# A four-layer graph network: where the next unit's row is spread in PSUM

## The chip, the cores and the metric

The kernel runs on one core of a Trainium2 chip. The metric is device microseconds (us) of one execution. A core has five engines that run side by side and wait for each other through semaphores: PE (TensorE, matrix products), DVE (VectorE), ACT (ScalarE), POOL (GpSimd) and SP (SyncE, which here issues DMAs). PE writes its results into PSUM; DVE and ACT read them there.

## The reference

The input is `x`, 8 images of 2048 nodes with 64 features, and `adj`, one 2048x2048 adjacency matrix that all images and layers share. Four layers follow each other, each as `x = layernorm(x + layer(x, adj))`.

Layers 0, 1 and 2 are graph attention. With `h = x @ W`, `s1 = h @ a1`, `s2 = h @ a2`:

```python
e = leaky_relu(s1[:, :, None] + s2[:, None, :], negative_slope=0.2)
att = softmax(where(adj > 0, e, very_negative), axis=-1)
out = att @ h          # then elu (layers 0, 1) or relu (layer 2)
```

Layer 0 scales the nodes first and normalizes `h`. Layer 3 has no scores between nodes: it takes `feat = softplus(...)`, weights it by `exp(feat * wa + ba)` and averages it over each node's neighbours, so it is one product of the mask with numerators and denominators.

## The kernel before, in words

**Units and tiles.** For layers 0 to 2 a unit is one image in one layer. The list `todo` has 24: layers 0 and 1 of images 0 to 3 (units 0 to 7), the same of images 4 to 7 (units 8 to 15), and layer 2 of all images (units 16 to 23). A unit has K = 16 tiles `jb`; a tile holds 128 neighbours (on the partitions) against all 2048 nodes (along the free axis). Layers 0 and 1 are "the first two layers" and layer 2 "the third layer" below.

**A tile.** `weights(u, jb)` is one DVE instruction: it takes the larger of the unit's row `r` and a number per partition, times the mask `edge`, and writes `w` (128x2048). The first and last tile of a unit are done in two halves (`halves`), so that what waits for one half can go on. In the third layer `exponential` then puts `w` through Exp on ACT; in the first two layers the weights are already exponentials. `products(u, jb)` multiplies the tile by the values (`pv`, or `x` in the third layer) on PE and adds into two PSUM banks `acc`; the profile counts two passes for fp32, so a tile has 8 matmul instructions. After the sixteenth tile four small matmuls add the mean for nodes without neighbours. There are 4 buffers for `w`.

**The row.** The row of a unit is the same on all partitions. It lies in DRAM as three bf16 parts whose sum is the fp32 value; `prepare` loads them into SBUF ahead of time, at step 10 of the unit before or later, as soon as they are ready. `spread` (line 830) brings them to all partitions: four matmuls of 128x512 with ones as the stationary operand write four PSUM banks, `r`. There is one such `r` for all units from 1 on (`psR`, one buffer). So a unit's row can be spread only when the last weights of the unit before have read the old one, and the next unit's first weights can start only after it.

**Order of the work.** All compute instructions go through `InOrder`, which keeps each engine's instructions in the order in which the program issues them; that helper is line 80 of the file, and the profile therefore shows line 80 for nearly all of them. DMAs on SP are placed by the framework.

The main loop goes over units and tiles. A step `t = K*n + jb` does this in order: `reach(t)`, `products(u, jb)`, possibly `prepare` for the next unit, and `bg.step()`. `bg.step()` advances the side work: generators for everything else (the end of the unit before, the next layer's scores, features of later images, in the third layer also layer 3's products `p_l`), each of which issues a piece per step.

`reach(t)` (line 1013) issues weights as far as they may run ahead of the products: in the first two layers those of tile `t`, in the third layer those up to tile `t + 2`. In the third layer it then issues exponentials up to tile `t + 1`. When it has issued a unit's last weights (`jb == K - 1`) and the next unit's row is prepared, it calls `spread_for(n + 1)` at once (line 1025). `spread_for` does nothing for a unit that has its row already; a unit whose row wasn't spread by then gets it just before its first weights.

So in the program's order, the spread stood after the last weights and before the sixteenth tile's products in the first two layers (step 15), and after the last weights and before the fourteenth tile's products in the third layer (step 13, since weights run two tiles ahead).

Of the kernel before, what the change touches and what calls it, by code (L numbers as in the profile page):

```python
# [50 lines left out]
def gnn4_kernel(ctx: ExitStack, tc: tile.TileContext, t, out):  # L51
# [3 lines left out]
    K = N // P  # L55
# [224 lines left out]
    def mask(p, jb):  # L280

        for h in range(2):
            dve.tensor_scalar(
                edge[:, jb, h * (N // 2) : (h + 1) * (N // 2)],
                raws[jb][h], 0.0, None, ALU.is_gt, saturate=False,
            )
        if jb < 6:
            load_raw(jb + 6)
        elif jb >= 10:
            load_raw(jb + 2)  # L290
        if jb == K2:
            load_x(2)
        if jb >= K - 3:
            load_x(jb - K + 6)
        if jb == 0:
            pe.matmul(p[:, : 2 * K], lhsT=edge[:, 0, :P], rhs=zeros_h, start=True, stop=False)
        for ib in range(K):
            pe.matmul(
                p[:, 2 * ib : 2 * ib + 2],
                lhsT=edge[:, jb, ib * P : (ib + 1) * P],  # L300
                rhs=ones_h,
                start=False,
                stop=False,
            )
        if jb == K - 1:
            pe.matmul(p[:, : 2 * K], lhsT=edge[:, 0, :P], rhs=zeros_h, start=False, stop=True)
# [21 lines left out]
    def empties(p):  # L328
        deg = p[:, : 2 * K : 2]
        dve.tensor_scalar(empty, deg, 0.0, None, ALU.is_equal)  # L330

        dve.tensor_scalar(
            half_ldeg, deg.bitcast(I32), 0.5 * LN2 / (1 << 23), LSE_UP - 63.5 * LN2,
            ALU.mult, ALU.add,
        )

        em = tmp.tile([P, 4, NCH, 32], F32, tag="oT", name="em")
        dve.tensor_copy(
            em,
            empty.rearrange("p (c k) -> p k c", k=4)[:, :, :, None].to_broadcast([P, 4, NCH, 32]),  # L340
        )
        q = Banks.pool.tile([P, 512], F32, tag="b", name="p_empty")
        for k in range(4):
            pe.transpose(
                q[:, k * P : (k + 1) * P], em[:, k].rearrange("p c b -> p (c b)"), ident
            )
        dve.tensor_copy(emptyT, q)
# [482 lines left out]
    def spread(layer, b):  # L830

        sc = S[layer, b]
        sc.r = Banks.r
        for c in range(NCH):
            sl = slice(c * 512, (c + 1) * 512)
            pe.matmul(sc.r[:, sl], lhsT=ones3, rhs=sc.r3[:, sl], start=True, stop=True)
# [134 lines left out]
    def unit(layer, b):  # L971
        u = Unit()
        u.layer, u.b, u.n = layer, b, f"{layer}_{b}"
        u.s, u.w = S[layer, b], {}
        return u

    def sums_of(u):
        u.acc = [psA.tile([P, 512], F32, tag="acc", name=f"acc_{u.n}_{c}") for c in range(2)]
# [5 lines left out]
    def weights(u, jb):  # L984

        s = u.s
        w = u.w[jb] = work.tile([P, N], F32, tag="w", name=f"w_{u.n}_{jb}", bufs=4)
        low = s.low if u.layer == 2 else s.e[:, 1]
        for sl in halves(u, jb):
            dve.scalar_tensor_tensor(  # L990
                w[:, sl], s.r[:, sl], low[:, jb : jb + 1], edge[:, jb, sl], ALU.max, ALU.mult
            )

    def exponential(u, jb):

        w = u.w[jb]
        for sl in halves(u, jb):
            act.activation(w[:, sl], w[:, sl], AF.Exp, bias=u.s.down[:, jb : jb + 1])

    units, prepared, spreads = [], set(), {0}  # L1000

    def spread_for(n):
        if n in spreads:
            return
        spreads.add(n)
        if n == 1:
            Banks.use("psR", 1)
            Banks.r = Banks.pool.tile([P, N], F32, tag="b", name="r")
        spread(*todo[n])
# [3 lines left out]
    def reach(t):  # L1013

        while front[0] < K * len(todo):
            n, jb = divmod(front[0], K)
            layer, b = todo[n]
            if n not in prepared or front[0] > t + (2 if layer == 2 else 0):
                break
            if jb == 0:  # L1020
                spread_for(n)
                units.append(unit(layer, b))
            weights(units[n], jb)
            front[0] += 1
            if jb == K - 1 and n + 1 in prepared:
                spread_for(n + 1)
        while behind[0] < min(front[0], t + 2):
            n, jb = divmod(behind[0], K)
            if todo[n][0] == 2:
                exponential(units[n], jb)  # L1030
            behind[0] += 1

    def products(u, jb):

        s, w = u.s, u.w[jb]
        sums = [u.acc[c // 2][F * (c % 2) : F * (c % 2) + F, :] for c in range(NCH)]
        for c in range(NCH):
            pe.matmul(
                sums[c],
                lhsT=s.v[:, jb, :],  # L1040
                rhs=w[:, c * 512 : (c + 1) * 512],
                start=(jb == 0),
                stop=False,
            )
        if jb == K - 1:

            assert s.whole
            for c in range(NCH):
                rows = slice(32 * c, 32 * c + 3)
                pe.matmul(sums[c], lhsT=s.mean[rows], rhs=emptyT[rows], start=False, stop=True)  # L1050
# [337 lines left out]
    def chain(*gens):  # L1388
        for g in gens:
            if isinstance(g, int):  # L1390
                yield g
            else:
                yield from g()
# [26 lines left out]
    def flags():  # L1420

        for layer in range(2):
            dve.tensor_scalar(s_top[:, layer], s_top[:, layer], -S_MAX[layer], None, ALU.add)
        top = small.tile([P, 2], F32, tag="top", name="top")
        dve.tensor_reduce(top[:, 0:1], s_top, AX.XY, ALU.max)
        yield 1
        yield from pm_slots.take()
        p = psum("p_top")
        pe.transpose(p[:1, :P], top[:, 0:1], ident)
        yield 1  # L1430
        dve.tensor_reduce(top[0:1, 1:2], p[:1, :P], AX.X, ALU.max)
        pm_slots.give()
        dve.tensor_tensor(beyond[0:1, :], beyond[0:1, :], top[0:1, 1:2], ALU.max)
        dve.tensor_scalar(flag, beyond[0:1, :], 0.0, None, ALU.is_gt)
# [3 lines left out]
    for n, (layer, b) in enumerate(todo):  # L1438
        if (layer, b) == (2, 1):
            early_.close()  # L1440
            late = ctx.enter_context(tc.tile_pool(name="late", bufs=1))
            bg.add(l3_products())
        if (layer, b) == (2, 5):
            bg.add(flags())
        now[:] = layer, n, 0
        nxt = todo[n + 1] if n + 1 < len(todo) else None
        done = nxt is None

        for jb in range(K):
            if n == 0:  # L1450
                while masks < min(K, 9 + jb):
                    mask(p_deg, masks)
                    masks += 1
                if jb == K - 3:
                    empties(p_deg)
            now[2] = jb
            reach(K * n + jb)
            u = units[n]
            if jb == 0:
                sums_of(u)  # L1460
            products(u, jb)
            if jb == K - 1:
                end = [lambda u=u: finish(u)]
                if layer < 2:
                    end += [2 if now[0] < 2 else 1, lambda layer=layer, b=b: scores(layer + 1, b)]
                else:
                    end += [1, lambda b=b: l3_features(b)]
                if layer == 1 and b % NB == NB - 1:
                    end += [lambda b=b: group(b // NB)]
                bg.add(chain(*end), begun=True)  # L1470
            elif not done and jb >= 10 and ready(*nxt):
                prepare(*nxt)
                prepared.add(n + 1)
                done = True
            if layer == 0 and jb == 2 and 6 <= b + 4 < B:
                load_x(b + 4)
            if n == 0 and jb == 3:
                bg.add(constants())
            if n == 9 and jb == 3:
                bg.add(mask_out())  # L1480
            if (n, jb) in begin:
                bg.add(features0(begin[n, jb]))
            bg.step()
        while not done:
            bg.step()
            if ready(*nxt):
                prepare(*nxt)
                prepared.add(n + 1)
                done = True
# [509 lines left out]
```

## Time and profile before

| What | Value |
|---|---|
| Median of 3 runs | 1397.81 us (1397.5 to 1398.58) |
| Profiled execution | 1401.63 us |
| Its span, first to last instruction | 1399.8 us |
| Mean granted PE clock | 0.951 |
| PE busy | 1220.0 us (87%) |
| DVE busy | 1208.8 us (86%) |
| ACT busy | 821.6 us (59%) |
| POOL busy | 770.2 us (55%) |
| Spread of rows, `r<-row,ones` on PE | 92 matmuls, median 374 ns, from 102.8 to 1159.0 us |

The span divides into an opening (to about 104 us), the first two layers (to 741 us), the third layer with layer 3's products beside it (to about 1222 us), and the rest of layer 3. "Busy" is the time in which an engine executes something. Matmuls are pipelined, so consecutive ones overlap in the profile by some 0.07 us, and a busy PE isn't PE at its peak. A group of instructions is named by what it writes and reads, as `w<-r,se,edge`; after the bar stand its busy time, the mean length of one, and the engine's idle time just before them with what ended it. In a timeline each row has start, length, engine, and in brackets the idle time before it.

### The profile page before, as it was taken

To read this page: it belongs to the slowest core of one execution; us is meant where nothing else is said; L and a number is where in the kernel's file an instruction comes from. 1 tells how busy PE (TensorE), PEld (TensorE's weight loads), DVE (VectorE), ACT (ScalarE), POOL (GpSimd) and SP (SyncE) were. 2 spreads that over 40 slices of the span, in tenths; PEclk is the share of its full clock that TensorE was granted. 3 is DMA by queue.
4 is the path that set the end of the run, shared out by engine and by line. 5 is a ranking of instruction groups with operands and counts; after the bars stand their busy time and mean duration, and the time that the engine had idled before them with its cause. 6 is when DMAs were issued, how large, how long until landed. Compare 5 with 4: busy or idle time off the path is not lost.

```text
span 1399.8 us, 19531 instructions
## 1 busy us (share of the span) xinstructions
PE 1220.0 (87%) x7169; PEld 624.2 (45%) x7169; DVE 1208.8 (86%) x1108; ACT 821.6 (59%) x1593; POOL 770.2 (55%) x1075
## 2 busy tenths in 40 slices
PE   3699888999898988999997879799989999976995
PEld 3333233333343333333332324256645565666995
DVE  3889889999997999889998888998879798877876
ACT  3444543666646753555547996868666758664432
POOL 1666776546765663645542342443555564776664
PEclk8699999999999999999999988999999899998998
DMA  8640000000000221222101000034543444511111
GB/s 291 228 95 1 1 2 1 1 2 1 3 1 1 91 76 47 78 74 93 32 1 39 1 15 1 22 94 129 146 122 92 127 119 138 160 28 33 35 38 34
DMA packets 112010, 87.24 MB, mean 62 GB/s; under 512 B 57917, under 2 KB 90845, under 8 KB 110882
## 3 DMA queue, kind: packets, MB, share of 16 engines
q1 hardware_dynamic: 111538, 85.79, 20.9%
q8 instruction: 59, 0.97, 0.3%
q14 instruction: 45, 0.37, 0.1%
q10 hardware_dynamic: 368, 0.12, 0.0%
HBM read 60.40 MB, written 25.45 MB: 61 GB/s over the span
## 4 chain that ended last, share of the span: by engine, by line
PE 49%; DVE 24%; ACT 11%; issue 7%; POOL 6%; DMA 2%; SPq 1%; ACTq 0%; DVEq 0%; POOLq 0%
PE acc L80 26%; DVE w L80 16%; PE p_l L80 14%; ACT w L80 2%; PE p_o L80 2%; ACT x L80 2%; DVE o L80 1%; PE r L80 1%; PE p_s L80 1%; POOL sq_x L80 1%; DMA raw<-in_adjT_dram 1%; DVE nd L80 1%; POOL st_x L80 1%; DVE edge L80 1%; ACT y L80 1%
## 5 line engine op out<-in xcount | busy, mean ns | idle before, releaser
L80 DVE SCALAR_TENSOR_TENSOR w<-r,se,edge 128x2048 f32<-128x2048 f32 (+1 forms) x270 | 552.9, 2102 | 30.9 <-PE r L80 22.6
L80 PE MATMUL acc<-w,pv 128*64 128x512 f32 x2048 | 494.1, 615 | 53.0 <-DVE w L80 39.4
L80 DVE SCALAR_TENSOR_TENSOR w<-r,lo_g,edge 128x2048 f32<-128x2048 f32 (+1 forms) x144 | 297.8, 2096 | 26.0 <-PE r L80 12.4
L80 ACT ACTIVATE w<-w,down_g 128x2048 f32<-128x2048 f32 (+1 forms) x144 | 256.8, 1808 | 64.6 <-DVE w L80 57.4
L80 PEld LDWEIGHTS p_l<-v,mask 128*128 128x128 f32 x2048 | 256.3, 196 | 61.8 <-issue 48.5
L80 PE MATMUL p_l<-v,mask 128*128 128x256 f32 x2048 | 271.1, 291 | 10.6 <-POOL mask L80 7.0
L80 PE MATMUL acc<-w,x 128*64 128x512 f32 x1024 | 261.8, 640 | 19.2 <-ACT w L80 16.3
L80 PEld LDWEIGHTS acc<-w,pv 128*64 128x64 f32 x2048 | 132.6, 139 | 307.6 <-issue 182.4
L80 POOL TENSOR_TENSOR sq_x<-sq_x 128x32 f32<-128x32 f32 (+4 forms) x207 | 110.1, 532 | 63.8 <-ACT sq_x L80 49.3
L80 PEld LDWEIGHTS acc<-w,x 128*64 128x64 f32 x1024 | 66.5, 143 | 138.9 <-issue 86.6
L80 ACT ACTIVATE x<-o,st_x 128x64 f32<-128x64 f32 x256 | 91.5, 445 | 13.2 <-POOL st_x L80 13.2
L80 ACT ACTIVATE nd<-p_l,empty 128x256 f32<-128x256 f32 x64 | 30.2, 471 | 109.1 <-PE p_l L80 109.1
L80 ACT ACTIVATE o<-p_o,den 128x64 f32<-128x64 f32 x256 | 55.8, 323 | 47.0 <-DVE den L80 47.0
L80 PE MATMUL p_o<-rh,oT 128*128 128x130 f32 x384 | 61.9, 298 | 24.4 <-DVE o L80 6.7
L80 PEld LDWEIGHTS p_o<-rh,oT 128*128 128x128 f32 x384 | 50.2, 197 | 58.3 <-issue 32.3
L80 ACT COPY oT<-acc 128x512 f32<-128x512 f32 x48 | 25.7, 587 | 80.8 <-PE acc L80 80.8
L80 POOL TENSOR_TENSOR st_x<-isw_x,mhalf 128x16 f32<-128x16 f32 x24 | 70.5, 2938 | 1.9
L80 POOL TENSOR_TENSOR eh<-eh,x 128x1024 f32<-128x1024 f32 (+2 forms) x24 | 36.5, 1532 | 47.0 <-ACT eh L80 47.0
L80 DVE RECIPROCAL nd<-nd 128x256 f32<-128x256 f32 x32 | 55.7, 1742 | 0.0
L80 POOL TENSOR_TENSOR d<-x,wa_bc 128x1024 f32<-128x1024 f32 x8 | 19.0, 2379 | 66.5 <-DVE x L80 66.5
L80 POOL TENSOR_TENSOR sq_x<-o 128x512 f32<-128x512 f32 x23 | 29.3, 1273 | 34.6 <-DVE o L80 34.1
L80 ACT ACTIVATE xs<-x,nodes 128x64 f32<-128x64 f32 x128 | 44.7, 434 | 3.2 <-PE p_xT L80 3.2
(258 smaller groups left out, 1523.5 us busy)
## 6 DMA issues: line engine op xcount, KB each, us to landing
mask<-mask_d SPq DMA_DIRECT2D x132, 256.0 KB
mask_d<-mf SPq DMA_DIRECT2D x32, 512.0 KB
raw<-in_adjT_dram SPq DMA_DIRECT2D x8, 1024.0 KB
raw<-in_adjT_dram SPq DMA_DIRECT2D x16, 512.0 KB
x<-in_x_dram SPq DMA_DIRECT2D x8, 512.0 KB
x_d<-x SPq DMA_DIRECT2D x8, 512.0 KB
e<-x_d SPq DMA_DIRECT2D x64, 64.0 KB
out_dram<-o SPq DMA_DIRECT2D x64, 64.0 KB
```

Source lines behind the costliest of these rows:

```text
L80: ins = f(*args, **kwargs)
```

## The change

The call of `spread_for` leaves `reach` and goes to the main loop, behind `products` and ahead of `prepare` and the side work. In the first two layers it comes after the fifteenth tile's products (`jb == K - 2`); since the last weights have to be issued first, `reach` is called there for the next step, so the sixteenth tile's weights also move ahead of the fifteenth step's side work. In the third layer it comes after the fourteenth tile's products (`jb == K - 3`); the last weights have been issued by then, and the call of `reach` there finds nothing to do.

```diff
@@ reach
             weights(units[n], jb)
             front[0] += 1
-            if jb == K - 1 and n + 1 in prepared:
-                spread_for(n + 1)
         while behind[0] < min(front[0], t + 2):
@@ main loop
             if jb == 0:
                 sums_of(u)
             products(u, jb)
+            if n + 1 in prepared and jb == K - (3 if layer == 2 else 2):
+                reach(K * n + jb + (0 if layer == 2 else 1))
+                spread_for(n + 1)
             if jb == K - 1:
                 end = [lambda u=u: finish(u)]
```

## The prediction

> **What bounds the kernel now.** I call the place where the kernel goes from unit k-1 to unit k hand-over k (units count from 0; a unit is one image in one of the first three layers, so there are 23). I first read the busy time by stage. The columns are the stretch, its length, then busy time and instruction count of PE, PE's weight loads, DVE, ACT and POOL, the granted clock, and DMA share and rate.
>
> ```profile
> 741.00:1222.00 481.00, 433.83 (x2526) 225.24 (x2526) 416.36 (x387) 360.81 (x346) 224.32 (x318) 0.94 0.31 87
> 104.00:741.00 637.00, 579.28 (x3062) 226.60 (x3058) 589.17 (x431) 340.31 (x1007) 384.04 (x563) 0.99 0.09 28
> ```
>
> In the first two layers (104 to 741 us) DVE is busy 589 of 637 us and PE 579, so both are near their bound; in the third layer (741 to 1222) PE leads with 434 of 481. So I asked what ends DVE's idle time in the first two layers, by groups with shapes kept apart (busy us, mean ns, then idle before and its releasers).
>
> ```profile
> L80 DVE SCALAR_TENSOR_TENSOR w<-r,se,edge 128x2048 f32<-128x2048 f32 x210 | 480.8, 2338 | 0.0
> L80 DVE SCALAR_TENSOR_TENSOR w<-r,se,edge 128x1024 f32<-128x1024 f32 x60 | 74.1, 1276 | 30.9 <-PE r L80 22.6 <-ACT mean L80 4.3 <-issue 4.0
> L80 DVE RECIPROCAL den<-p_o 128x4 f32<-128x4 f32 x60 | 7.9, 164 | 6.2 <-PE p_o L80 4.7 <-issue 1.0
> ```
>
> The 210 whole tiles never wait. The 60 half tiles, which are the first and last of a unit, hold 30.9 us of DVE's 48 idle us: DVE stands at each hand-over until PE has spread the next row. The timeline of PE and then of DVE at hand-over 9 shows it (start, length, idle before).
>
> ```profile
> 442.06 2.74 PE L80 MATMUL acc<-w,pv 128*64 128x512 f32 x12
> 444.74 1.09 PE L80 MATMUL p_xT_2v<-ident,x 128*128 128x128 f32 x8
> 445.76 1.03 PE L80 MATMUL r<-row,ones 3*128 3x512 bf16 x4
> 446.72 1.94 PE L80 MATMUL acc<-w,pv 128*64 128x512 f32 x8
> ...
> 446.83 4.74 DVE L80 SCALAR_TENSOR_TENSOR w<-r,se,edge 128x1024 f32<-128x1024 f32 x3 [3.05 <-PE r L80]
> ```
>
> DVE is done with the old row at 443.78. PE is still in the fifteenth tile's products (to 444.81), then does 1.0 us of side work, then the spread. In the third layer the spread stands ahead of the fourteenth tile's products, and there it can hold PE up (timeline at hand-over 22):
>
> ```profile
> 1085.01 2.17 PE L80 MATMUL p_l<-v,mask 128*128 128x256 f32 x16
> 1088.06 1.02 PE L80 MATMUL r<-row,ones 3*128 3x512 bf16 x4 [0.87 <-DVE w L80]
> 1089.01 3.34 PE L80 MATMUL acc<-w,x 128*64 128x512 f32 x8
> ```
>
> [...] nothing of PE runs in the 0.87 us above. [...] the spread can't start before the old row's last reader ends; at hand-overs 10, 11 and 14 it starts 0.05 us after it. [...] Here the granted clock was 0.50 from 891.5 to 898.2, around an idle stretch of 5.80 us at hand-over 19, and 0.50 from 1089.5 to 1092.7, which explains the 3.34 us above where 8 such matmuls else take 1.94.
>
> **The change part by part.** It adds and removes nothing: a spread stays four matmuls of 128x512, 1.03 us. Instruction order on DVE, ACT and POOL is the same, since the side work of the fifteenth step holds no DVE instruction in layers one and two. SP's queue shows a few swaps: the row load for unit 21 passes two 64 KB loads, and three others move by one place; none is near its use, I price them at nothing. On PE the order changes at 9 hand-overs of the first two layers (2, 3, 6, 7, 8, 9, 12, 13, 16: spread before side work) and at all 7 of the third (17 to 23: spread behind the fourteenth tile's products). At 1, 4, 5, 10, 11, 14 and 15 that step has no PE side work and nothing moves.
>
> First two layers: the spread can start at the later of the end of the fifteenth tile's products and 0.05 us after DVE's last read. Against the trace this is earlier by 0.37 (behind p_mean), 1.26 (p_s), 1.20 (p_h), 0.58, 1.02, 1.02, 0.51 (p_xT), 0.39 (p_lse) and 1.26 (p_s): 7.6 us that DVE could start earlier. PE itself wins nothing: side work and spread change places and the sixteenth products come at the same time, and at 7, 12 and 13 they come 0.44 us later, because PE now waits for DVE's last read where it did side work before. So DVE keeps a lead only as far as it doesn't run into results of PE, ACT or POOL that come no earlier. Unit by unit, from how long such inputs had lain ready in the trace:
> Hand-over 2: DVE waits 2.37 us for POOL's st_h at 162.84 anyway: 0. Hand-over 3: s_top's input lay ready 1.03 us at 195.25: 1.03, and PE, which waits for DVE in eight later tiles, follows. 6: den's input lay ready 1.00 at 327.30: 1.00, carried on by the chain den, ACT o, POOL o. 7: den at 368.2 waits for PE already: 0; the 0.44 is hidden, since p_o waits 0.84 for ACT at 367.48. 8: mean waits 3.12 for ACT at 426.85: 0. 9: den had 0.64 at 461.08: 0.64. 12: PE is the chain from 574 to 604 without a gap: -0.44. 13: the chain goes from the spread to DVE: +0.39. 16: the chain goes through the sixteenth products and ACT's copy: 0. Sum 2.6 us.
>
> Third layer: PE does the products (1.94 us) first, so where PE came late the next unit's first weights come 1.94 later. Behind them wait their exponentials on ACT. At 20 DVE then waits 2.22 us for ACT before x<-x,sp, at 21 0.60 and 6.48, at 23 2.58, and these waits take it up:
>
> ```profile
> 960.31 1.23 DVE L80 TENSOR_TENSOR x<-x,sp 128x1024 f32<-128x1024 f32 x1 [2.22 <-ACT x L80]
> ```
>
> At 17 ACT's first two exponentials move by 1.0, and ACT then idles 1.09 before the copy out of the sums: 0. Without these covers the four cost up to 7.8. Where DVE came late, PE fills its wait: at 22 it saves 0.87, and PE is the chain there; at 19 the products must wait for an exponential that ends at 890.76, can then use the idle time before 893.42, and the next products end some 0.45 earlier; at 18 the wait of 0.94 is filled, but the first weights move from 839.01 to 839.9, and with them lim_g, te and the second exponential: about -0.4. Sum 0.9 us.
>
> Total 2.6 + 0.9 = 3.5 us. The profiled execution took 1401.63 us (span 1399.8), which gives 1398.1; the median of the runs is 3.8 us below that execution, and I take the same difference: 1397.8 - 3.5 = 1394.3.
>
> **The rivals.** *DVE keeps all it gains*: 7.6 + 0.9 = 8.5 us, 1389.3. For it: DVE's whole tiles never wait. Against it: PE is 91% busy in these stages and den had under 1.2 us to spare in most units. *It is swallowed*: each lead ends at the next den or mean, and PE's 0.44 us stalls eat the rest; 1397.8, within 2. For it: three of the nine hand-overs are certainly of that kind. *Slower by late weights in the third layer*: if ACT's softplus chain comes earlier than in this trace, the covers at 20 and 23 fall below 1.94 us (now 2.22 and 2.58, so 0.3 and 0.6 us decide), DVE's delay goes through, and 17 and 18 add theirs; three of 1.94 and 0.9 at 18 is 6.7, less the 2.6 gained before: +4, 1402. For it: DVE is on the chain at 1036 to 1041 and 1170 to 1187. Against it: PE lags these weights by 3 to 8 us in most tiles.
>
> **How the numbers follow.** Forecast 0.40 (1392 to 1396), all kept 0.15, swallowed 0.27, slower 0.18. Faster by over 0.2% (2.8 us, about what a measurement of this kernel can tell from no change) 0.55, same 0.27, slower 0.18. The range runs from the all-kept end to inside the slower case: 1389.5 to 1400.5; the forecast's own is 1392 to 1396. A half-clock window of 3.4 us more or less on PE is worth 1.7 us, and the range holds two.
>
> **What would show it.** Idle before the half tiles of the first two layers falls from 30.9 to about 24; den and mean waits grow by 3 to 5 us. At hand-over 9 the spread follows the acc matmuls at once. In the third layer acc comes ahead of r, DVE's idle before the first weights grows at 17, 20, 21 and 23, and the wait before x<-x,sp shrinks by as much. I am wrong if DVE's waits on p_o grow by as much as those on r shrink, if x<-x,sp ends later than before, or if the half-clock windows differ by more than two.

## The result, and the profile after

The changed kernel takes 1391.2 us (median of 6 runs, 1388.84 to 1393.72); the kernel before, beside it, 1398.19 us (6 runs). The ratio is 0.9948, 95% interval 0.9926 to 0.997: faster by 7 us, or half a percent. Timed twice more in the experiments it gave 0.9967 (0.9954 to 0.9979) and 0.997 (0.9961 to 0.998), which is 4.6 and 4.2 us of 1397. The profiled execution took 1393.72 us with a span of 1391.9, against 1401.63 and 1399.8 before.

Busy time by stage in the kernel after (columns as before: stretch, length, then busy time and count of PE, PE's weight loads, DVE, ACT and POOL, granted clock, DMA):

```profile
104.00:741.00 637.00, 584.12 (x3056) 228.18 (x3052) 592.10 (x432) 340.14 (x1007) 382.99 (x563) 0.97 0.09 28
741.00:1222.00 481.00, 433.75 (x2562) 226.84 (x2563) 415.24 (x388) 364.22 (x350) 226.47 (x321) 0.96 0.30 89
```

DVE and PE are both busy for a little longer in the first stage (592.1 and 584.1 against 589.2 and 579.3), but part of PE's increase is only that its clock fell from 0.99 to 0.97, and at a granted clock of 0.50 matmuls are busy for longer (in the kernel before 3.34 us for the 8 behind the spread at hand-over 22, against 1.94 here). In the third layer the clock went the other way, from 0.94 to 0.96.

DVE's groups by shape in the first two layers (busy us, mean ns, idle before and its releasers); the last line is that of the means in the kernel before:

```profile
L80 DVE SCALAR_TENSOR_TENSOR w<-r,se,edge 128x1024 f32<-128x1024 f32 x60 | 74.1, 1275 | 24.3 <-PE r L80 18.2 <-issue 6.0
L80 DVE SCALAR_TENSOR_TENSOR mean<-mean,later,mean 128x64 f32<-128x64 bf16 x40 | 23.4, 585 | 4.7 <-ACT mean L80 4.7
L80 DVE RECIPROCAL den<-p_o 128x4 f32<-128x4 f32 x60 | 8.4, 167 | 8.7 <-PE p_o L80 7.3 <-issue 1.0
```

```profile
L80 DVE SCALAR_TENSOR_TENSOR mean<-mean,later,mean 128x64 f32<-128x64 bf16 x40 | 21.4, 535 | 3.9 <-ACT mean L80 3.9
```

The half tiles wait 6.6 us less (24.3 against 30.9). The reciprocals and the means wait 3.3 us more (8.7 and 4.7 against 6.2 and 3.9). The means are also 2.0 us longer busy (23.4 against 21.4); what is behind that comes with the third profile below. Hand-over 9 in the timeline of PE and then of DVE:

```profile
440.82 3.65 PE L80 MATMUL acc<-w,pv 128*64 128x512 f32 x16
444.41 1.03 PE L80 MATMUL r<-row,ones 3*128 3x512 bf16 x4
445.37 1.09 PE L80 MATMUL p_xT_2v<-ident,x 128*128 128x128 f32 x8
446.39 1.94 PE L80 MATMUL acc<-w,pv 128*64 128x512 f32 x8
...
445.48 6.99 DVE L80 SCALAR_TENSOR_TENSOR w<-r,se,edge 128x1024 f32<-128x1024 f32 x4 [1.71 <-PE r L80]
```

The spread follows the products at once, the side work has taken its place, and DVE waits 1.71 us where it waited 3.05. The sixteenth products begin at 446.39, after spread and side work as before: PE has won nothing by itself.

In the third layer the products now stand ahead of the spread (timeline of PE at hand-over 22):

```profile
1085.29 1.94 PE L80 MATMUL acc<-w,x 128*64 128x512 f32 x8
1087.16 1.03 PE L80 MATMUL r<-row,ones 3*128 3x512 bf16 x4
1088.12 2.18 PE L80 MATMUL p_l<-v,mask 128*128 128x256 f32 x16
```

PE no longer stands still there, and the half-clock window behind it is gone: the granted clock was 0.50 from 1089.5 to 1092.7 us before, and is 1.00 from 1041 to 1234 us now. What DVE waited for in the third layer (741 to 1222 us; total us, times, longest), first before, then after:

```profile
DVE x L80 <- ACT x L80: 19.5, 6, 7.0
DVE w L80 <- PE r L80: 12.4, 5, 3.8
```

```profile
DVE w L80 <- PE r L80: 20.7, 6, 5.7
DVE x L80 <- ACT x L80: 13.4, 6, 5.6
```

The first weights of a unit wait 8.3 us longer in all, and the sum of x and sp waits 6.1 us less: the delay goes into a wait that was there already. At hand-over 20 the sum begins at 959.92 with 0.35 us of waiting, where it began at 960.31 with 2.22; counted from the sum `x<-x,d` at 905 us in each trace that is 0.16 us earlier, so nothing of the delay is left.

### The profile page after: what moved, and what is told of

Read it like the earlier page. It is cut to its first block, busy times and chain, and to the rows that moved or that the text cites. A ratio compares the mean times of both kernels' runs of the same rounds, so it can differ in the third digit from the quotient of the medians.

```text
span 1391.9 us, 19529 instructions
## 1 busy us (share of the span) xinstructions
PE 1216.6 (87%) x7169; PEld 621.8 (45%) x7169; DVE 1210.8 (87%) x1108; ACT 821.7 (59%) x1593; POOL 767.1 (55%) x1075
## 4 chain that ended last, share of the span: by engine, by line
PE 46%; DVE 24%; ACT 13%; POOL 7%; issue 6%; DMA 3%; SPq 2%; DVEq 0%; POOLq 0%; ACTq 0%
PE acc L80 25%; DVE w L80 14%; PE p_l L80 14%; ACT w L80 3%; DMA raw<-in_adjT_dram 2%; ACT x L80 2%; DVE o L80 2%; PE p_o L80 2%; PE p_s L80 2%; PE r L80 1%; ACT sp L80 1%; DVE nd L80 1%; POOL st_x L80 1%; DVE x L80 1%; POOL sq_x L80 1%
## 5 line engine op out<-in xcount | busy, mean ns | idle before, releaser
L80 DVE SCALAR_TENSOR_TENSOR w<-r,se,edge 128x2048 f32<-128x2048 f32 (+1 forms) x270 | 552.9, 2101 | 24.3 <-PE r L80 18.2
```

The costliest lines, as they stand in the source:

```text
L80: ins = f(*args, **kwargs)
```

## The experiments

The twelve runs fall into three series, each on a chip of its own and beside the kernel before, whose median in the three was 1396.25, 1396.42 and 1396.24 us; between series only the ratios can be compared. A difference of 0.001 in a ratio is 1.4 us. Since no kernel here changes the order on DVE, the same DVE instructions mark the same places in every trace. The table gives the length of each stretch in us and in brackets the part of it at half clock, worked out from the traces. The marks, all of them DVE instructions, are the first half tile of unit 1, that of unit 16, the sum `x<-x,d` at 905 us, the reduction `st<-o` at 1264 us and the reduction `st<-sq` at 1325 us (times of the kernel before).

| Profile of | first two layers | to 905 | 905 to 1264 | 1264 to 1325 |
|---|---|---|---|---|
| before | 637.2 (17) | 163.9 (34) | 358.6 (27) | 61.5 (14) |
| before, second time | 637.7 (24) | 163.8 (34) | 358.7 (27) | 61.5 (14) |
| first two layers only | 637.8 (34) | 163.3 (34) | 352.7 (17) | 61.4 (14) |
| the same again | 636.4 (34) | 163.8 (31) | 355.7 (20) | 61.4 (14) |
| third layer only | 639.0 (34) | 165.0 (27) | 352.8 (17) | 59.9 (14) |
| the same again | 637.1 (20) | 162.0 (31) | 352.9 (17) | 59.9 (14) |
| after | 636.9 (34) | 164.9 (31) | 352.9 (14) | 59.9 (14) |
| after, second time | 635.7 (34) | 165.0 (31) | 352.8 (17) | 59.9 (14) |
| after, third time | 636.3 (20) | 162.6 (24) | 352.9 (14) | 59.9 (14) |
| third from unit 18 on | 636.2 (20) | 162.2 (24) | 354.5 (20) | 61.5 (14) |
| third until unit 17 | 637.8 (34) | 163.4 (24) | 352.8 (17) | 61.4 (14) |
| third one tile later | 637.0 (34) | 165.2 (31) | 354.1 (17) | 61.4 (14) |
| first two behind the sixteenth | 659.2 (58) | 163.3 (27) | 352.9 (17) | 59.9 (14) |
| first two ahead of the fifteenth | 663.8 (62) | 164.3 (30) | 352.8 (14) | 59.9 (14) |

**The first pair of traces misled me.** DVE's lead over the kernel before (how much earlier it starts the same instruction) was -0.03 us after hand-over 15 and 4.1 us at hand-over 23. I read from it that the first two layers give nothing and the third layer everything (Theory A below), with chance in the clock as the rival (Theory B). The first series tests this.

**The changed kernel again.** No edit.

> The changed kernel once more, on the chip of the next three runs. Two theories of its gain of 7.0 us. Theory A (place): the third layer's move keeps PE fed, so after unit 22 DVE is ahead of the kernel before by 4 to 6 us in every profile, whatever the clock did. Theory B (clock): of the 7 us about half is that the profile of before had four half-clock windows between 985 and 1222 us and the profile after one, by chance; then a second profile of the changed kernel shows two or more half-clock windows there, and the lead after unit 22 is 2 us or less. The time is expected at 1391 (1389 to 1394) by both, since both have to give the median of six runs.

Measured: 1391.82 us, ratio 0.9967 (0.9954 to 0.9979). The lead at hand-over 23 was 3.2 us, with two half-clock stretches between 985 and 1222 us. Neither theory has it: less than A asked for and more than B allowed, and B's two stretches are there. (The kernel before, profiled a second time, later differed from its own first profile by up to 3.5 us at hand-over 18, so a lead of this size in one pair of traces says little.)

**Only the first two layers.**

```diff
@@ reach
+            if jb == K - 1 and n + 1 in prepared and layer == 2:
+                spread_for(n + 1)
@@ main loop
-            if n + 1 in prepared and jb == K - (3 if layer == 2 else 2):
-                reach(K * n + jb + (0 if layer == 2 else 1))
+            if n + 1 in prepared and layer < 2 and jb == K - 2:
+                reach(K * n + jb + 1)
                 spread_for(n + 1)
```

> Only the move in layers one and two (behind the fifteenth tile's products); the third layer's spread stands where it stood before. Theory A (the gain comes from the third layer; in the first two it is swallowed, as DVE's lead after hand-over 15 was -0.03 us): 1397 (1396 to 1398.5), within 1.5 us of before. My prediction's split: 2.6 us faster, 1395.2. Rival (DVE keeps its leads of the first two layers and the trace hid it): 5 us or more faster, 1393 or less.

Measured: 1393.41 us, ratio 0.9974 (0.9959 to 0.9989), 3.6 us of 1397. Theory A's number falls: moved alone, the first two layers give a gain, and near what the prediction's sum had for them. But in this profile and in its repetition the first two layers themselves are hardly shorter (637.8 and 636.4 us against 637.2 and 637.7, with more half clock); the gain shows between 905 and 1264 us.

**Only the third layer.**

```diff
@@ reach
+            if jb == K - 1 and n + 1 in prepared and layer < 2:
+                spread_for(n + 1)
@@ main loop
-            if n + 1 in prepared and jb == K - (3 if layer == 2 else 2):
-                reach(K * n + jb + (0 if layer == 2 else 1))
+            if n + 1 in prepared and layer == 2 and jb == K - 3:
+                reach(K * n + jb)
                 spread_for(n + 1)
```

> Only the move in the third layer (behind the fourteenth tile's products); layers one and two as before. Theory A: nearly the whole gain, 6 us faster, 1391.5 to 1393. My prediction's split: 0.9 us faster, 1397. Theory B (clock by chance): about 3 us faster, 1394 to 1396. Slower than before would mean that late weights cost more than PE saves, and that the gain lies in the first two layers.

Measured: 1392.97 us, ratio 0.9972 (0.9958 to 0.9985), 3.9 us. It is more than the prediction's 0.9 and less than A's 6.

**The third layer without hand-overs 17 and 18,** with the first two layers as in the changed kernel.

```diff
@@ reach
+            if jb == K - 1 and n + 1 in prepared and 16 <= n < 18:
+                spread_for(n + 1)
@@ main loop
-            if n + 1 in prepared and jb == ...
+            if n + 1 in prepared and not 16 <= n < 18 and jb == ...
```

> As the changed kernel, but hand-overs 17 and 18 keep the old place of the spread (ahead of the fourteenth tile's products), where the changed kernel's trace lost 3.3 us of DVE's lead at the first weights of units 17 and 18. If that loss is real and carried: faster than the changed kernel by 2 to 3 us, 1388 to 1389.5. If it is made good at once (DVE's reciprocals for unit 17 at 861 to 866 us were again 1.05 us ahead of before): equal to the changed kernel within 1 us, 1390 to 1392. If instead those two hand-overs made the gain: slower than the changed kernel by 1 us or more.

Measured: 1393.95 us, ratio 0.9979 (0.9967 to 0.9991). It is slower than the changed kernel by 2.1 us (the two intervals overlap), though the changed kernel's trace is 3.3 us behind the kernel before at just these two places, and ahead again by 1.1 us at 19. Taken alone this says that the third layer's gain is made at 17 and 18. The counterpart asks for it. (In both edits the dots stand for the rest of the line as in the change.)

**The third layer until unit 17 only.**

```diff
@@ reach
+            if jb == K - 1 and n + 1 in prepared and n >= 18:
+                spread_for(n + 1)
@@ main loop
-            if n + 1 in prepared and jb == ...
+            if n + 1 in prepared and n < 18 and jb == ...
```

> As the changed kernel, but hand-overs 19 to 23 keep the old place of the spread; 17 and 18 and the first two layers have the new one. With both moves the gain was 4.4 us, with 17 and 18 left in the old place 2.3. Theory D (the third layer's gain is made at 17 to 19): as the changed kernel within 1 us, 0.9965 (0.995 to 0.998). Prediction's split (0.87 at 22 and 0.45 at 19 gained, 0.4 lost at 18): like the first two layers alone or slower, 0.9978 or more. Theory C (one hand-over more or less can't be told from the clock's spread): anywhere from 0.9965 to 0.998.

Measured: 1395.94 us, ratio 0.9989 (0.9975 to 1.0002). Theory D isn't borne out. Neither part of the third layer's move has the gain of the whole (0.9967): with a part of the hand-overs moved, the kernel ends no better than with the first two layers alone. A sum over hand-overs fits this poorly, though the intervals overlap. The table's last column shows one piece of the gain, 1.5 us that only profiles with all seven moved have.

**The kernel before, against itself.** No edit.

> The kernel before, once more, timed against itself and profiled a second time. Theory C (the clock's share is a matter of where the work falls on the clock's 3.4 us windows, and it differs from execution to execution): the ratio is 1 within 0.2%, and the second profile's stretch from 902 us to 1256 us, which took 358.6 us in the first profile and 352.7 to 354.4 us in four others, some with the same order of instructions there, takes 352 to 355 us. If the first profile was no accident and the old place of the spread costs this, it takes 357 us or more again.

Measured: 1395.52 us, ratio 0.9998 (0.9978 to 1.0017), no difference, as it should be. The stretch from 905 us took 358.66 us, as in the first profile: Theory C's number falls. Two profiles of the same kernel agree within 0.1 us and hold the same 27 us at half clock. The stretch in the kernel before, in the one with the first two layers alone, whose instructions stand in the same order there, and in the kernel after:

```profile
905.02:1263.61 358.59, 333.19 (x1963) 203.15 (x1959) 304.52 (x305) 242.90 (x217) 193.93 (x262) 0.96 0.41 113
```

```profile
905.78:1258.51 352.73, 328.88 (x1963) 201.49 (x1959) 304.16 (x305) 242.59 (x217) 194.60 (x262) 0.98 0.40 115
```

```profile
904.79:1257.66 352.87, 327.62 (x1963) 201.74 (x1959) 303.80 (x305) 242.65 (x217) 194.49 (x262) 0.98 0.40 115
```

The counts of work are the same, DVE's and ACT's busy times agree within 0.3%, and the clock is 0.96 in the long one and 0.98 in the others. With the spread in its old place this stretch took 352.7, 352.8, 355.7, 358.6 and 358.7 us in five profiles (17, 17, 20, 27 and 27 us of it at half clock); with all seven moved it took 352.8 to 352.9 in seven of seven (14 to 17 us). So at the like clock the move is worth nothing here. With all seven moved the stretch was always short, with the old place in two of five profiles: whether the move keeps it short is likely by these numbers, not shown.

The two profiles of the kernel before also aren't typical of it. They are executions of 1401.63 and 1401.54 us; its median is 1396, and only 17 of the 181 executions beside the three series took 1401.5 us or more. No trace shows one near the median, so that the stretch differs from execution to execution, which was Theory C's idea, isn't excluded. Leaving out every execution above 1398 us, the medians still differ by 3.4 us for the whole change, 2.2 for the first two layers alone and 2.3 for the third alone (all series together). So the long stretch of these two traces can't be the whole gain, and what the rest is stays open.

**How the clock went with a wait.** The last stretch shows it in the small. In every one of the fourteen traces PE waits 2.35 us for ACT's conversion of a mask. PE's clock changes in steps of 3.41 us, here called windows; they begin at another place of the kernel in each trace. Three such windows in the kernel before, then in the kernel after:

```profile
1294.21:1297.62 3.41, 2.94 (x25) 2.73 (x23) 3.38 (x7) 2.62 (x7) 2.41 (x4) 1.00 0.18 41
1297.62:1301.04 3.42, 1.54 (x13) 1.55 (x14) 3.42 (x5) 1.82 (x2) 3.36 (x2) 1.00 0.00 0
1301.04:1304.45 3.41, 3.41 (x19) 3.41 (x18) 3.14 (x10) 0.78 (x2) 0.12 (x2) 0.50 0.14 31
```

```profile
1289.43:1292.84 3.41, 1.62 (x14) 1.42 (x12) 3.38 (x7) 3.41 (x6) 2.51 (x4) 1.00 0.08 19
1292.84:1296.25 3.41, 2.85 (x23) 2.85 (x24) 3.31 (x4) 0.51 (x1) 2.21 (x2) 1.00 0.00 0
1296.26:1299.66 3.40, 3.40 (x31) 3.40 (x30) 1.92 (x8) 2.90 (x4) 1.24 (x2) 1.00 0.34 77
```

Before, 1.88 us of the wait falls into one window, and the next is granted 0.50: PE does 19 products in it. After, the wait is split 1.79 and 0.57 between two windows, and the next runs at 1.00 with 31 products. Over all traces the larger part of this wait is 1.88 us or more in seven, and in all seven half clock follows; it is 1.79 or less in the other seven, and none follows. The seven are just those with 61.4 to 61.5 us in the last column. Both groups have 14 us at half clock there, but in the short ones all of it lies ahead of this wait, which takes the delay up. Behind the wait nothing takes it up: followed back from the end of the kernel, what decides the time from here on is PE alone for 704 products (start, length), before and after:

```profile
1299.49 86.24 PE p_l L80 x704
```

```profile
1293.40 84.75 PE p_l L80 x704
```

The difference of 1.49 us is the price of the lost window, nearly all of the 1.6 between the two groups.

The lost products also shift POOL's conversion of the next mask, and it falls onto a DVE instruction. Before (POOL, then DVE), and then after:

```profile
1308.99 1.94 POOL L80 CAST mask<-edge 128x2048 fp32r<-128x2048 fp8e4 x1 [1.33 <-PE p_l L80]
1309.28 1.93 DVE L80 TENSOR_TENSOR o<-o,e 128x256 f32<-128x256 f32 x1
```

```profile
1303.78 0.42 DVE L80 TENSOR_TENSOR o<-o,e 128x256 f32<-128x256 f32 x1
1309.12 2.15 DVE L80 TENSOR_TENSOR o<-o,e 128x256 f32<-128x256 f32 x1
```

Beside the conversion the sum takes 1.93 us, alone 0.42. But this isn't where the 1.6 us come from: in the kernel after, the next such sum meets a conversion and takes 2.15 us (0.43 before), in all seven traces of its group.

**The third layer one tile later.**

```diff
-            if n + 1 in prepared and jb == K - (3 if layer == 2 else 2):
+            if n + 1 in prepared and jb == K - 2:
```

> The third layer's spread stands one tile later than in the changed kernel, behind the fifteenth tile's products, so that the first weights of the next unit come about 4 us later at each of hand-overs 17 to 23 (1.94 us of products and 2.17 us of the mask's products, where these run). Rival 'late weights decide': the waits before the sum of x and sp (2.22 and 2.58 us left at 20 and 23) no longer cover, three to five hand-overs lose 2 to 4 us each, 8 to 15 us slower than the changed kernel (1400 to 1407 beside 1391.8). Theory of the prediction (PE lags behind the weights by 3 to 8 us in most tiles and hides it): slower than the changed kernel by 0 to 4 us, 1392 to 1396.

Measured: 1396.32 us, ratio 0.9993 (0.9981 to 1.0005). Against the changed kernel's 0.9967 that is 3.6 us, at the upper end of what the prediction's reasoning gave. The rival's 8 us and more do not come. But the gain over the kernel before is gone. DVE's waits before the sum of x and sp are now 0 at hand-overs 20 and 23 (0.35 and 0.72 us in the changed kernel): behind the fourteenth tile's products these covers hold, behind the fifteenth's they are used up. How much of the 3.6 us that is isn't shown, since 1.5 us of the two traces' difference lies behind 1264 us, where the two kinds of trace above differ by as much.

**The first two layers behind the sixteenth tile's products.**

```diff
-            if n + 1 in prepared and jb == K - (3 if layer == 2 else 2):
-                reach(K * n + jb + (0 if layer == 2 else 1))
+            if n + 1 in prepared and jb == K - (3 if layer == 2 else 1):
+                reach(K * n + jb)
```

> In layers one and two the spread goes behind the sixteenth tile's products, so that DVE starts the next unit's first half tile some 2.35 us later (1.94 us of products, 0.41 us of the sums' matmuls) than behind the side work, at up to 16 hand-overs. It measures what share of a shift in DVE's start goes through to the end. If all of it goes through, 37 us slower than before (1434). If the share is the one my prediction had (2.6 of 7.6 us, a third), 12 to 13 us slower (1409). If it is hidden as the first pair of traces made it look (DVE's lead after hand-over 15 was -0.03 us), within 3 us of before (1394 to 1400).

Measured: 1417.99 us, ratio 1.0138 (1.0111 to 1.0165), 19.3 us slower than before and 23.9 slower than the changed kernel (1.0138 less 0.9967). DVE's half tiles in the first two layers:

```profile
L80 DVE SCALAR_TENSOR_TENSOR w<-r,se,edge 128x1024 f32<-128x1024 f32 x58 | 71.6, 1276 | 62.6 <-PE r L80 46.5 <-ACT oT L80 11.9 <-issue 4.2
```

They wait twice as long as before (62.6 against 30.9), 31.7 us more, and the kernel ends 19.3 us later. That excludes that the place of the spread is hidden. What share of a late start of DVE goes through it doesn't tell: half clock in the first two layers rose to 58 us from the 17 and 24 of the kernel before, and by my estimate, which takes half of the time at a granted 0.50 as lost, those 34 to 41 us more are 17 to 20 us of PE's time.

**The first two layers ahead of the fifteenth tile's products.**

```diff
+            if layer < 2 and jb == K - 2 and n + 1 in prepared:
+                reach(K * n + jb + 1)
+                spread_for(n + 1)
             products(u, jb)
-            if n + 1 in prepared and jb == K - (3 if layer == 2 else 2):
-                reach(K * n + jb + (0 if layer == 2 else 1))
+            if n + 1 in prepared and jb == K - 3 and layer == 2:
+                reach(K * n + jb)
                 spread_for(n + 1)
```

> In layers one and two the spread stands ahead of the fifteenth tile's products instead of behind them; the third layer as in the changed kernel. DVE can start the next unit up to 1.9 us earlier where it waited for PE, but PE now stands idle until DVE has read the old row for the last time (0.9 us at hand-over 9 by the trace of before: 443.83 less 442.87), and the fifteenth products come later by that and by the spread. If DVE's start is what counts, with the share of 0.55 that the move to behind the sixteenth showed (20 us for 37): some 1 us at up to 16 hand-overs, 5 to 9 us faster than the changed kernel, 1383 to 1387. If PE's products count as much: equal or slower by up to 5 us, 1392 to 1397. A clear loss would say that behind the fifteenth is the right place.

Measured: 1419.02 us, ratio 1.0167 (1.0144 to 1.019): 27.5 us slower than the changed kernel, which no theory had so large. DVE's groups in the first two layers, then PE's:

```profile
L80 DVE SCALAR_TENSOR_TENSOR w<-r,se,edge 128x1024 f32<-128x1024 f32 x57 | 70.5, 1276 | 19.3 <-PE r L80 17.0 <-issue 2.4
L80 DVE RECIPROCAL den<-p_o 128x4 f32<-128x4 f32 x58 | 9.2, 175 | 30.9 <-PE p_o L80 29.8 <-issue 1.0
```

```profile
L80 PE MATMUL r<-row,ones 3*128 3x512 bf16 x56 | 17.1, 430 | 24.8 <-DVE w L80 20.3 <-DMA row<-row_d 4.4
```

DVE's wait for the spread does fall, from 24.3 to 19.3. But PE now stands 24.8 us ahead of the spreads, of that 4.4 for the row's load, and DVE waits for PE's later results instead: the reciprocals 30.9 us where the changed kernel has 8.7. The wait has mostly changed its name, and PE has lost time. Here too the half-clock time of these layers is high, 62 us, and how much of the 27.5 us it makes wasn't separated.

**Both halves and the whole, once more.** No new edits.

> The changed kernel a third time, beside the two halves of the change, each a second time. Theory E (both halves gain on their own, and most of what the first pair of traces hid or showed too much is half-clock windows): 0.9967 within 0.0015; its stretch from 902 to 1256 us takes 352.8 to 352.9 us as in the two profiles so far, and units 0 to 8 take 342 to 343 us with 20 to 24 us at half clock.

> Only layers one and two, again. Theory E and my prediction's first sum (2.6 us): 0.998 (0.9972 to 0.9988). If the first result (0.9974) was luck and these layers give nothing: 0.9990 or more.

> Only the third layer, again. Theory E (it takes the slow clock patterns away; executions above 1398 us, 3 in 10 of the kernel before, are gone): 0.9972 (0.996 to 0.998), at most 1 in 10 executions above 1398. My prediction's 0.9 us: 0.9994 (0.9988 or more).

Measured: 0.997 (0.9961 to 0.998) for the whole, 0.9988 (0.9973 to 1.0003) for the first two layers, 0.998 (0.9971 to 0.999) for the third. The stretch from 905 us took 352.9 us, as expected; from unit 1's first half tile to unit 9's, which is what the expectation calls units 0 to 8, it took 341.7 us with 7 us at half clock, less than expected in both. In two results each, the first two layers give 3.6 and 1.7 us (the second one's interval reaches 1), the third layer 3.9 and 2.8, and both together 4.6 and 4.2. Of executions above 1398 us the kernel before has 53 of 181, the first two layers alone 8 of 44, the third layer alone 0 of 40, the whole 1 of 44. Theory E's number holds for the third layer, and the executions above 1398 us are gone with it. That the halves add up (some 6 us) to more than the whole lies within these intervals; I can't tell whether it is real.

This third profile allows a comparison that the others don't. From unit 1 to hand-over 13 its half-clock windows lie at the same places of the kernel as those of the first profile of the kernel before, within 0.1 us; so do those of the second profile of the third layer alone, which has the old place in the first two layers, but for one more in unit 2. Counted from unit 1's first half tile, DVE's lead over the kernel before is 1.31 us at hand-over 3 but 0.04 at 4, 1.26 at 6 but 0.33 at 7, 1.23 at 9 but 0.21 at 11, and 0.12 at 13. (The profile of the third layer from unit 18 on, with the same windows, agrees to about 0.1.) With the old place it is 0.1 or less throughout. Where the lead goes at 3 and 6 isn't a wait: DVE's mean takes longer (1.62 us for 0.63, and 1.70 for 0.52). At hand-over 6 before (DVE, then POOL), and in the third profile of the kernel after:

```profile
319.89 0.52 DVE L80 SCALAR_TENSOR_TENSOR mean<-mean,later,mean 128x64 f32<-128x64 bf16 x1
317.96 2.36 POOL L80 TENSOR_TENSOR o<-o,eh 128x1024 f32<-128x1024 f32 x1
```

```profile
319.10 1.70 DVE L80 SCALAR_TENSOR_TENSOR mean<-mean,later,mean 128x64 f32<-128x64 bf16 x1
318.35 2.36 POOL L80 TENSOR_TENSOR o<-o,eh 128x1024 f32<-128x1024 f32 x1
```

DVE comes to the mean earlier, but the mean ends only 0.09 us after POOL's sum in both. In all eight profiles with the new place in the first two layers this mean takes 1.69 to 1.71 us. The longer mean at hand-over 3 lies beside another POOL instruction.

## Why the prediction was right, and where not

**The sum.** Forecast 3.5 us faster, 1394.3. The first result is 7.0 us faster, 1391.2, inside the range and 0.8 us below the forecast's own; the two later ones are 4.6 and 4.2. The direction and the size of the whole hold; the composition doesn't, so that the sum came out near is in part luck.

**First two layers, 2.6 us: the size fits, the terms don't.** Timed alone they gave 3.6 and 1.7. The idle time before the half tiles was to fall to about 24 and is 24.3; den and mean were to wait 3 to 5 us longer and wait 3.3 longer; hand-over 9 looks as described. But the terms that make up the 2.6, 1.03 at 3, 1.00 at 6 and 0.64 at 9, were to be kept, and where the half-clock windows are alike (the third profile) 0.1 us of lead is left at hand-over 13. The prediction looked for results that DVE would have to wait for, and took the length of its instructions as given; the means beside POOL's work became longer (1.62 us for 0.63 at 3, 1.70 for 0.52 at 6), and the lead went there. The terms at 12 and 13 come out: -0.05 together, and DVE's lead changes by -0.1 from 11 to 13. Hand-over 16 was put at 0. There DVE starts 1.26 us earlier, and in the two profiles of the first two layers alone it has gained 1.9 and 1.4 us from unit 15's start to 905 us; as the half-clock windows differ, that isn't proof. By which way the rest of the 3.6 and 1.7 us comes stays open. The rival that DVE keeps all of its 7.6 us falls with the intervals of these two runs, which end at 5.7 and 3.8 us; the rival that all is swallowed falls with the intervals of the whole, which end at 0.998 and below, though up to hand-over 13 it describes the traces better than the forecast.

**Third layer, covers: right.** The waits before the sum of x and sp took up most of what the first weights lost (6.1 of 8.3 us). The rival of late weights was a tile away: one tile later the covers at 20 and 23 are used up.

**Third layer, 0.9 us: this step failed.** I priced PE's filled stalls, 0.87 at 22 and 0.45 at 19, less 0.4 at 18. At the like clock the stretch that holds hand-overs 19 to 23 is no shorter than before (352.7 and 352.9 us), and the one with 17 and 18 neither (163.3 to 163.9 against 162.0 to 165.0). Timed alone the third layer gave 3.9 and 2.8 us. The traces show two differences that stand in no term. One goes with PE's clock: the stretch from 905 to 1264 us has 23 us at half clock in the mean of four profiles with the third layer as before (both of before, both with the first two layers only), and 15.6 in seven with all of it moved, which is 356.4 and 352.9 us. The other is 1.6 us between 1264 and 1325 us, one half-clock window on PE's chain of products, far from any line that the change touches. Together they are 5.1 us, more than was timed, and two of the four profiles are those executions of the kernel before at 1401.5 us; so they show where the gain can lie, and not its full account.

**The clock, as a spread of two windows: wrong.** I had written that I am wrong if the half-clock windows differ by more than two. They did: 136 us before and 123 after in the first pair (mean granted clock 0.951 and 0.956), some four windows. I took the clock for an accident that averages out. Where the windows begin did differ from trace to trace. But what followed the wait of 2.35 us went with how it fell into them: half clock in seven of seven traces with 1.88 us or more of it in one window, in none of seven with 1.79 or less. And the executions above 1398 us nearly vanish with the change (53 of 181 before, 1 of 44 with it).

## What to carry to other kernels

Where two engines are both near their bound, moving one instruction mostly renames the wait: look for the next result that the engine which gave way has to deliver, and take as kept only what lay ready ahead of that. Look also at what runs beside the instructions that come earlier: here a short mean that began earlier took 1.70 us instead of 0.52 and still ended 0.09 us after POOL's sum. Judge a change of half a percent by repeated timing, and compare stretches of a trace only at the like clock; one pair of traces misled me here. Ask also where the traced execution lies among the timed ones. Look at PE's short waits too, even off the critical path: here a wait of 2.35 us with 1.88 us in one window was followed by a window at half clock, and the products behind it took 1.49 us longer.

## What the runs showed of the hardware

Half clock came also after windows in which PE had worked: in the kernel before PE was busy for 1.54 us of the 3.42 from 1297.62, and the next window was granted 0.50. My counts over the fourteen traces of this kernel and its variants, with those of the first traces of before and after in brackets: a full-speed window in which PE was busy for less than 0.4 was followed by half clock in 218 of 218 cases (30 of 30); between 0.4 and 0.5 in 32 of 63 (5 of 11); above 0.5 in 64 of 4743 (9 of 683). In 18 of these 64 (3 of the 9) the profile shows PE busy for nearly the whole window, always with small products of four columns (`p_s`) among the others; why half clock follows there stays open. A window at half clock with PE busy below 0.7 was followed by another in 142 of 142 (23 of 23), from 0.7 to 0.8 in 27 of 32 (4 of 5), from 0.8 to 0.9 in 11 of 34 (3 of 6), and above in 10 of 296 (2 of 40). The bounds between the groups are only those of this count; that the clock goes by them isn't shown.

The wait of 2.35 us in the last stretch shows both outcomes: with 1.88 us of it in one window the next was granted 0.50 (before), with 1.79 and 0.57 us in two the next were granted 1.00 (after).

From 905 to 1264 us the seven profiles with all of the third layer moved took 352.8 to 352.9 us, although the stretch ahead of it differed from 162.0 to 165.0 us, while those with the old place took 352.7 to 358.7. What holds the seven together wasn't shown.

A DVE sum of 128x256 took 1.93 us beside POOL's conversion of a 128x2048 mask and 0.42 without it, in seven traces each: 1.5 us more for this sum. A DVE mean of 128x64 took 0.52 us when it met the end of a POOL sum of 128x1024, and 1.70 when it met more of it. What makes DVE's instruction longer there wasn't shown.
